# Local and global attention with a spectral feed-forward: loads on one queue, local denominators on TensorE alone, a layernorm's moments in the attention's slots

## The chip, the cores and the metric

The kernel runs on one core of a Trainium2 chip. The metric is the device time of one execution in microseconds. A core has a matrix engine (TensorE, PE in the profile; its weight loads are PEld), a vector engine (VectorE, DVE), an activation engine (ScalarE, ACT), a general engine (GpSimd, POOL) and a sync engine (SyncE, SP), each working through its own list of instructions in order. DMAs are issued from the lists of ACT and SP here, by instructions that can wait for semaphores like any others.

## What is computed

The input x is 2 x 8192 x 512 in float32. There are 16 heads of 32 channels and windows of 64 tokens.

```
y   = layernorm(x);  q, k, v = y @ w_qkv
loc = softmax(q . k of 64 keys around each query, 32 before to 31 after) @ v
glo = softmax(q . k of every 64th token of the whole sequence) @ v
x   = x + layernorm((loc + glo) @ w_out + b_out)
f   = real(ifft(fft(layernorm(x)) @ w_freq)) + bias
x   = x + layernorm(f)
```

The layernorms have no gain or shift. The Fourier transforms are folded into one 512 x 512 matrix at the start of the kernel, and matrix products split their operands into a high and a low part, three passes each.

## The kernel before

The program has three stages. The first projects q, k and v for 32 chunks of 512 tokens and stores them in DRAM (`qkd`, `kgd`, `vd`). The second is the attention, the third the residual and the feed-forward.

**Attention.** The work is cut into 128 units: 32 chunks times 4 groups (c) of 4 heads. The loop of line 884 runs over slots s. In one slot pieces of several units are laid out in the order of the string PLAN (line 822), which is an order written out by hand, and every engine follows it in its own list. The pieces are:

- `L0`, `L1`, `L2` (`load_unit`, line 147): four loads of queries (`qs`) and keys (`ks`) for unit s+3, issued from ACT's list (lines 167 and 169; line 173 for the global keys of a sequence's first chunk).
- `S` (`scores`, line 183), sixteen times: scores of unit s+2 on PE into one of three PSUM buffers, then two maxima on DVE (lines 200 and 203). `ne` (line 207) negates all the maxima at the slot's end, giving `mm`.
- `mx`, `sm`, `fm` for unit s+1: `mm` is transposed on PE (`pm`), copied on ACT (`mr`), stored from SP to DRAM (`md`, line 227) and loaded into four spare rows of `qs` (line 231). The load waits for the store.
- `g0`..`g3`, `a0`..`a3`, `b0`, `b1`, `k0`, `k1` for unit s: the products of the softmax on PE (into two PSUM buffers), their exponentials on ACT (line 625), and on POOL the selection of the window (line 675). The tile of local exponentials is `ptl`, that of global ones `ptg`.
- `ng`, `dg`, `n-`, `n0`..`n3`, `p0`, `p1`, `dl`, `de` for unit s-1: numerators and denominators. Denominators are matmuls with columns of ones. Each query has its local keys in two key blocks, so there are three pieces of `ptl` to be added. `p0` and `p1` (`gather`, line 727) first add two of them into `ptd`, one pair of heads on DVE and one on POOL; `dl` and `de` (`den_l`, line 737) then feed one piece of `ptl` and `ptd` to PE, 4 matmuls each.
- `dT`, `dI`, `t0`, `t1` on DVE (lines 761 to 775): the denominators are turned, inverted and spread (`dt`, `rc`, `rb`). `c0`, `c1`, `c2` on POOL multiply and add (`num`, `att`).
- `hs`, `ls`, `o0`..`o3`, `oe`, `ot` (class `Project`, line 787): a block of 128 tokens of an earlier chunk is split on ACT (`ath`) and DVE (`atl`), multiplied by `w_out` on PE (`po`; the third matmul of each three needs `atl`), given its bias on DVE (`t`, line 812) and stored from SP to DRAM (`td`, line 815).
- `va`, `vb`, `vc`: loads of the next chunk's values (`vh`, `vt`) from SP, in every fourth slot.

The PLAN of before:

```
L0 S S oe mx g0 L1 S S g1 p1 p0 a0 L2 ot c1 sm ng vg dg S S S a1 hs b0 k0 ls c2 S S va
n- n0 n1 n2 fm n3 dl de S S S g2 dT dI g3 vb t0 o0 S a2 o1 c0 S a3 t1 vc S o2 b1 k1 S o3 ne
```

After the last unit, the pieces that are left go into the list `rest`.

**Feed-forward.** 128 blocks of 128 tokens in groups of four go through nine steps (line 1066), one block a step, so that nine blocks and more are under way. `measure` takes the moments of the attention's output (`bn_stats` and `bn_aggr`, lines 108 and 109) from `t3r`, a ring of three chunks loaded from `td`, and POOL makes r1 and m1 of them at the group's end (`after_measure`, line 945). `residual` (line 989) adds to x, held in `x3r`, a ring of six chunks, and takes the moments of the sum. Then come `normalize` (ACT), `transpose` (PE, `pt`), `halves` (ACT `xh`, DVE `xl`), `ffn` (12 matmuls, `pf`), `last` (DVE), `spread` (ACT, squares) and `finish` (ACT, then an addition on POOL, line 1048). The last block of a chunk stores it (line 1054) and then loads the ring's next chunk into the place (line 915), which waits for the store. GAPS gives the least distance between steps of a block; a step in BATCHED waits for its whole group; PLACES orders the steps within one. Five pieces of `rest` are issued after each step.

Of the kernel before, what the change touches and what calls it, by code (L numbers as in the profile page):

```python
# [25 lines left out]
TB = 512  # L26
NB = TB // P
WIN = P + W
# [3 lines left out]
def kernel(  # L32
# [29 lines left out]
    nc = tc.nc  # L62
    B, N, C = x.shape
    DH = C // H
    KC = C // P
    R = P // DH
# [5 lines left out]
    KG = BACK + TB + HALF  # L72
    KW = KG + NG
# [11 lines left out]
    qkd = [[dram.tile([R, 4, DH, N], F32, name=f"qkd_{b}_{c}") for c in range(KC)] for b in range(B)]  # L85
    kgd = [dram.tile([KC, R, 2, DH, NG], F32, name=f"kgd_{b}") for b in range(B)]
# [19 lines left out]
    def stats(pool, mv, src, name):  # L106
        bs = pool.tile([P, 6], F32, tag="bs", name=f"bs_{name}", bufs=4)
        nc.vector.bn_stats(bs, src)
        nc.vector.bn_aggr(mv, bs)
# [4 lines left out]
    NU = len(units)  # L114
# [7 lines left out]
    ks, qbufs = [], []  # L122
# [24 lines left out]
    def load_unit(u, g):  # L147

        if not inside(u):
            return  # L150
        b, n, c = units[u]
        qs = QS[u] = qbufs[u % len(qbufs)]
        lo, hi = n * TB - BACK, (n + 1) * TB + HALF
        a, z = max(lo, 0), min(hi, N)
        if g == 0:
            if a > lo:
                nc.gpsimd.memset(ks[c][0:96, :, K0 : K0 + a - lo].bitcast(F32), 0.0)
            if z < hi:
                nc.gpsimd.memset(ks[c][0:96, :, K0 + z - lo : KG].bitcast(F32), 0.0)
        def heads(d, i, m):  # L160

            return d[:, i : i + m].rearrange("r i d t -> (i d) r t")

        def load(rows, i, m):
            rows = slice(rows, rows + m * DH)
            if i < 2:
                nc.scalar.dma_start(out=qs[rows].bitcast(F32), in_=heads(qkd[b][c][:, :, :, n * TB : (n + 1) * TB], i, m))
                return
            nc.scalar.dma_start(
                out=ks[c][rows, :, K0 + a - lo : K0 + z - lo].bitcast(F32), in_=heads(qkd[b][c][:, :, :, a:z], i, m)  # L170
            )
            if n == 0:
                nc.scalar.dma_start(out=ks[c][rows, :, KG:KW].bitcast(F32), in_=heads(kgd[b][c], i - 2, m))

        if g == 0:
            load(0, 0, 2)
        elif g == 1:
            load(DH, 2, 2)
        else:
            load(2 * DH, 0, 1)  # L180
            load(0, 2, 1)
# [54 lines left out]
    with ExitStack() as cx:  # L236
# [8 lines left out]
        xs, raw, spread, xT, kgs = {}, {}, {}, {}, {}  # L245
# [67 lines left out]
        with tc.tile_pool(name="setup", bufs=1, side="right") as sp:  # L313
# [124 lines left out]
            for d in range(KC):  # L438
# [3 lines left out]
                m = sp.tile([P, 2, C], F32R, tag="wf", name=f"wf_{d}")  # L442
# [3 lines left out]
                    out=wfd[:, d * P : (d + 1) * P, :].rearrange("i p o -> p i o"), in_=m.bitcast(F32)  # L446
# [6 lines left out]
        wk = cx.enter_context(tc.tile_pool(name="wk", bufs=2, side="right"))  # L453
# [116 lines left out]
    with ExitStack() as cx:  # L570
# [10 lines left out]
        ones = keep.tile([P, 2, DH], F32, name="ones")  # L581
# [31 lines left out]
        class Softmax:  # L613
# [4 lines left out]
            def __init__(self, u):  # L618
                self.u = u
                self.b, self.n, self.c = units[u]  # L620
                self.g, self.l, self.d = ([None, None] for _ in range(3))
                PT[u] = self

            def exp(self, dst, src):
# [99 lines left out]
                if m == NB - 1:  # L724
                    nc.scalar.copy(NUM[self.u][:, 1], self.nl)

            def gather(self, pair, eng):

                l = self.l[pair]
                d = self.d[pair] = wk.tile([P, 2, NB, W], F32, tag="ptd", name=f"ptd_{self.u}_{pair}", bufs=2)  # L730

                def part(at):
                    return bass.AP(tensor=l.tensor, offset=l.offset + at, ap=[l.ap[0], [WIN, 2 * NB], [1, W]])

                eng.tensor_tensor(d.rearrange("p i m w -> p (i m) w"), part(0), part(W), ALU.add)

            def den_l(self, half):

                ps = DEN[self.u].rearrange("p (m w) -> p m w", w=P)
                for r in range(R):  # L740
                    if half:
                        l = self.l[r // 2][:, r % 2]
                        rhs = bass.AP(tensor=l.tensor, offset=l.offset + 2 * W, ap=[l.ap[0], [WIN, NB], [1, W]])
                    else:
                        rhs = self.d[r // 2][:, r % 2]
                    nc.tensor.matmul(  # L746
                        ps[r * DH : (r + 1) * DH, :, half * W : (half + 1) * W],
                        ones[:, 1],
                        rhs,
                        start=False,  # L750
                        stop=True,
                        skip_group_check=True,
                    )

        class Finish:

# [30 lines left out]
        class Project:  # L787
# [22 lines left out]
            def bias(self):  # L810
                self.t = keep.tile([P, C], F32, tag="po", name=f"t_{self.i}", bufs=1)
                nc.vector.tensor_tensor(self.t, self.po, bo, ALU.add)

            def store(self):
                nc.sync.dma_start(out=td[self.k][self.j * P : (self.j + 1) * P, :], in_=self.t)

# [3 lines left out]


        PLAN = """
            L0 S S oe mx g0 L1 S S g1 p1 p0 a0 L2 ot c1 sm ng vg dg S S S a1 hs b0 k0 ls c2 S S va
            n- n0 n1 n2 fm n3 dl de S S S g2 dT dI g3 vb t0 o0 S a2 o1 c0 S a3 t1 vc S o2 b1 k1 S o3 ne
        """
        ENG = {k: nc.vector if e == "v" else nc.gpsimd for k, e in (t.split("=") for t in "p0=v p1=p c0=p c1=p c2=p".split())}
        plan = PLAN.split()
        wo = weights(keep, wod, "wo")
        bo = bias(keep, b_out, "bo")
        FIN = {}  # L830

        def slot(s):
# [20 lines left out]
            if inside(s - 1):  # L853
                v = PT.pop(s - 1)
                f = FIN[s - 1] = Finish(s - 1)
                ops |= {"ng": v.num_g, "dg": v.den_g, "n-": lambda: v.num_l(-1)}
                for m in range(NB):
                    ops[f"n{m}"] = lambda m=m: v.num_l(m)
                ops |= {"dl": lambda: v.den_l(1), "de": lambda: v.den_l(0)}
                for pair in range(R // 2):  # L860
                    ops[f"p{pair}"] = lambda pair=pair: v.gather(pair, ENG[f"p{pair}"])
                ops |= {"dT": f.turn, "dI": f.invert, "t0": lambda: f.spread(0), "t1": lambda: f.spread(1)}
                ops["c0"] = lambda: f.combine(0)
            if inside(s - 2):
# [7 lines left out]
                    ops[f"o{c}"] = lambda c=c: o.part(c)  # L872
            if inside(s - LAG - 1):
                z = PO.pop(s - LAG - 1)
                ops |= {"oe": z.bias, "ot": z.store}
            return ops

        LAG = KC + 2
# [20 lines left out]
    with ExitStack() as cx:  # L899
# [21 lines left out]
        class Group:  # L921
# [20 lines left out]
                nc.gpsimd.tensor_tensor(m, mv[:, :, 0:1], r, ALU.mult)  # L942
                return m

            def after_measure(self):
                self.r1 = self.rstd("r1", self.mv1[:, :, 1:2])
                self.m1 = self.moved("m1", self.mv1, self.r1)

            def after_residual(self):
                self.r2 = self.rstd("r2", self.mv2[:, :, 1:2])  # L950
# [15 lines left out]
        class Block:  # L966
# [14 lines left out]
                if self.i == self.g.n - 1:  # L981
                    getattr(self.g, f"after_{what}")()

            def measure(self):
                self.t = tring[self.k % len(tring)][:, self.j]
                self.stats("mv1", self.t)
                self.end("measure")

            def residual(self):
                self.x1 = xring[self.k % len(xring)][:, self.j]  # L990
                nc.vector.scalar_tensor_tensor(self.x1, self.t, self.g.r1[:, self.i], self.x1, ALU.mult, ALU.add)
                self.stats("mv2", self.x1)
                if self.j == NB - 1:
                    load_t3(self.k + len(tring))
                self.end("residual")
# [67 lines left out]
        groups = [Group(k, a, b) for k in range(NK) for a, b in zip(cuts[k], cuts[k][1:])]  # L1063
        blocks = [blk for g in groups for blk in g.blocks]

        STEPS = "measure residual normalize transpose halves ffn last spread finish".split()
        GAPS = dict(zip(STEPS, (0, 3, 2, 1, 1, 1, 1, 1, 2)))
        BATCHED = ("residual", "normalize", "spread", "finish")
        when, before = {}, [0] * len(blocks)
        for step in STEPS:  # L1070
            for i, blk in enumerate(blocks):
                at = i if step == "measure" else before[i] + GAPS[step]
                if step in BATCHED:
                    at = max(at, max(before[blocks.index(o)] for o in blk.g.blocks) + GAPS[step])
                if i and step != "measure":
# [6 lines left out]
        PLACES = "measure ffn halves last finish normalize spread residual transpose".split()  # L1082
# [95 lines left out]
```

## Time and profile before

| | us |
|---|---|
| median of 3 runs | 3813.4 (3806.15 to 3817.37) |
| profiled execution, its own time | 3819.91 |
| its span | 3818.2 |

Busy time over the span: PE 3462.0 us (91%), DVE 2591.0 (68%), POOL 1980.1 (52%), ACT 1664.8 (44%). The chain of waits follows the first stage's matmuls until 1080.9 us, and the attention's slots run from about 1131 to 3207 us. The feed-forward's first residual starts at 3270.7 us, the last one at 3768.8. In the profile L12 is line 12 of the kernel, a row `out<-in` names tiles with buffer numbers left out, and an idle time stands in square brackets with what ended it. A "chain of waits" is followed back from the last instruction of a stretch: at each step to what released it. "Busy PE" is modelled from the starts of matmuls, so it isn't PE at its peak. A float32 matmul stands in the trace as two records. "issue" is time in which an engine waited for nothing that the profile shows.

### The profile page before, as it was taken

The page shows a single profiled execution, that of the slowest core. Times are in us where ns is not written, and L with a number is a line of the kernel's source. Part 1 is how long each engine was busy: PE and PEld are TensorE (multiplying, and loading weights), DVE is VectorE, ACT ScalarE, POOL GpSimd, SP SyncE. Part 2 cuts the span into 40 slices and gives each one's busy share as a digit, 9 for nine tenths or more (in the row PEclk, how much of TensorE's full clock was granted, in tenths as well). Part 3 has the DMA queues.
Part 4 walks back from the last instruction along what each step waited for, and adds up shares of the span by engine and source line. Part 5 has one row for each costly group of instructions (what it writes and reads, how often), then busy time and mean ns, then how long its engine had stood idle before and what let it go on. Part 6 is the DMA issues. An engine that isn't in the chain of part 4 may idle for free.

```text
span 3818.2 us, 68772 instructions
## 1 busy us (share of the span) xinstructions
PE 3462.0 (91%) x23168; PEld 2569.3 (67%) x23168; DVE 2591.0 (68%) x9200; ACT 1664.8 (44%) x3711; POOL 1980.1 (52%) x2233
## 2 busy tenths in 40 slices
PE   7999999999997889998999989999989998788886
PEld 5778787888875566666666666666666665566665
DVE  5444344444445777777778877777778786788985
ACT  2222222222223445454545445454545454366666
POOL 2222222222213666666666666666666667266667
PEclk8999999999997999999999999999999999799998
DMA  7887887888876565656666565656565654355553
GB/s 236 236 240 233 238 243 235 240 238 238 240 207 167 127 153 148 160 147 153 154 149 159 143 148 148 157 149 156 147 161 147 161 146 136 119 188 200 198 199 131
DMA packets 355100, 685.05 MB, mean 179 GB/s; under 512 B 29729, under 2 KB 43681, under 8 KB 354242
## 3 DMA queue, kind: packets, MB, share of 16 engines
q1 hardware_dynamic: 244930, 454.13, 38.4%
q10 hardware_dynamic: 109824, 226.53, 25.4%
q8 instruction: 191, 3.13, 0.4%
q14 instruction: 155, 1.27, 0.1%
HBM read 436.08 MB, written 244.45 MB: 178 GB/s over the span
## 4 chain that ended last, share of the span: by engine, by line
PE 47%; DVE 25%; DMA 15%; ACT 4%; POOL 3%; SPq 2%; issue 2%; ACTq 1%; DVEq 0%; POOLq 0%
PE pp L98 15%; PE pv L98 6%; DVE junk L203 6%; PE s L199 5%; DVE mx L200 4%; DMA td<-t 4%; PE nl L693 4%; DMA x3r<-in_L_attn_x_dram 4%; DVE rb L775 4%; DMA out_dram<-x3r 3%; PE pa L628 3%; PE ng L693 3%; PE po L98 2%; PE den L693 2%; PE den L746 2%
## 5 line engine op out<-in xcount | busy, mean ns | idle before, releaser
L675 POOL TENSOR_SCALAR_AFFINE_SELECT ptl<-ptl 128x512 f32<-128x512 f32 (+1 forms) x768 | 629.3, 834 | 549.3 <-ACT ptl L625 531.8
L200 DVE TENSOR_REDUCE mx<-s 128x1 f32<-128x128 f32 x2048 | 576.8, 282 | 304.5 <-PE s L199 263.5
L203 DVE CUSTOM_DVE_ANT_0 junk<-s,mask 128x192 f32<-128x192 f32 x2048 | 709.7, 347 | 0.0
L98 PE MATMUL pp<-xT,wh 128*128 128x512 f32 x2048 | 649.4, 398 | 27.9 <-ACT xT L304 22.1
L199 PE MATMUL s<-ks,qs 96*128 96x384 f32 x1536 | 475.8, 381 | 82.4 <-DVE mx L203 74.6
L199 PEld LDWEIGHTS s<-ks,qs 96*128 96x128 f32 x1536 | 273.4, 191 | 321.7 <-issue 134.3
L780 POOL TENSOR_TENSOR num<-num,rb 128x512 f32<-128x512 f32 x256 | 386.1, 1508 | 177.3 <-DVE rb L775 177.3
L98 PEld LDWEIGHTS pp<-xT,wh 128*128 128x128 f32 x2048 | 388.6, 191 | 121.2 <-ACT xT L304 27.0
L625 ACT ACTIVATE ptl<-pa 128x384 f32<-128x384 f32 (+1 forms) x1024 | 337.2, 382 | 268.8 <-PE pa L628 254.4
L462 DVE TENSOR_TENSOR qk<-pp,qk 128x512 fp32r<-128x512 f32 x256 | 176.1, 689 | 380.9 <-ACT qk L461 372.4
L98 PE MATMUL pp<-xT,wl 128*128 128x512 f32 x1024 | 404.4, 395 | 0.0
L461 ACT CAST qk<-pp 128x512 fp32r<-128x512 f32 x256 | 149.6, 586 | 578.6 <-PE pp L98 415.3
L465 POOL CAST kgs<-qk 128x16 fp32r<-128x16 f32 x128 | 50.3, 393 | 669.9 <-DVE qk L462 669.9
L98 PE MATMUL po<-wo,ath 128*128 128x512 f32 x1024 | 350.6, 425 | 2.0 <-ACT ath L796 2.0
L625 ACT ACTIVATE ptg<-pg 128x512 f32<-128x512 f32 x512 | 276.4, 586 | 172.3 <-PE pg L628 169.9
L98 PE MATMUL pf<-wf,xh 128*128 128x512 f32 x1024 | 336.5, 410 | 0.0
L98 PE MATMUL pv<-wh,xT 128*128 128x512 f32 x1024 | 322.4, 390 | 0.0
L628 PEld LDWEIGHTS pa<-qs,ks 128*128 128x128 f32 x1536 | 242.8, 201 | 105.7 <-ACT ptg L625 90.7
L628 PE MATMUL pa<-qs,ks 128*128 128x192 f32 (+1 forms) x1536 | 254.0, 276 | 41.7 <-ACT ptg L625 41.0
L98 PE MATMUL pf<-wf,xl 128*128 128x512 f32 x512 | 215.6, 421 | 53.2 <-DVE xl L1012 47.6
L297 POOL TENSOR_TENSOR xt<-xt,spread 128x512 f32<-128x512 f32 x128 | 177.3, 1394 | 161.4 <-DVE xt L296 160.8
L98 PE MATMUL po<-wo,atl 128*128 128x512 f32 x512 | 213.1, 416 | 24.9 <-DVE atl L800 24.9
(161 smaller groups left out, 6831.6 us busy)
## 6 DMA issues: line engine op xcount, KB each, us to landing
qkd<-qk SPq DMA_DIRECT2D x512, 256.0 KB
ks<-qkd ACTq DMA_DIRECT2D x112, 640.0 KB
qs<-qkd ACTq DMA_DIRECT2D x128, 512.0 KB
ks<-qkd ACTq DMA_DIRECT2D x112, 320.0 KB
x<-in_L_attn_x_dram SPq DMA_DIRECT2D x32, 1024.0 KB
xt<-in_xt_dram SPq DMA_DIRECT2D x32, 1024.0 KB
vd<-v SPq DMA_DIRECT2D x128, 256.0 KB
qs<-qkd ACTq DMA_DIRECT2D x128, 256.0 KB
```

What stands on the lines that cost most here:

```text
L98: nc.tensor.matmul(ps, w, m, start=start and i == 0, stop=stop and i == len(terms) - 1)
L199: nc.tensor.matmul(ps[:, 0:w].rearrange("p (i w) -> p i w", i=2), q, both, start=True, stop=True)
L200: nc.vector.tensor_reduce(mx[:, j, 0, r : r + 1], ps[:, w - NG : w], AX.X, ALU.max)
L203: nc.vector.tensor_tensor_reduce(junk, ps[:, 0:WIN], fixed["mask"][:, variant, :], 1.0, LOWEST, ALU.add, ALU.max, mx[:, j, 1, r : r + 1])
L297: nc.gpsimd.tensor_tensor(t, t, r, ALU.mult)
L462: nc.vector.tensor_tensor(st[:, 2 * is_k + 1], pp, st[:, 2 * is_k], ALU.subtract)
L625: nc.scalar.activation(dst, src, AF.Exp, scale=SCALE)
L628: nc.tensor.matmul(ps, ks[self.c][:, r, lo : lo + m], QS[self.u][:, r, q0 : q0 + w], start=True, stop=True)
L675: nc.gpsimd.affine_select(part(at, w), part(at, w), [[0, 8], [step, w]], ALU.is_ge, 0.0, base=base, channel_multiplier=-step)
L693: nc.tensor.matmul(ps[r * DH : (r + 1) * DH, at], lhsT, rhs, start=start, stop=True, skip_group_check=True)
L775: nc.vector.transpose(self.rb[:, g], self.rc[:, g].unsqueeze(2).to_broadcast([P, TB // DH, DH]))
L780: ENG[f"c{g}"].tensor_tensor(num[:, g], num[:, g], self.rb[:, g], ALU.mult)
```

## The change

All loads of `load_unit` are issued from SP's list. `gather` is gone with `ptd`: `den_l` runs 12 matmuls, one for each of four heads and three pieces of `ptl`. The moments of the attention's output are taken in the slot, right from `t` in SBUF (`om`), and kept for all 128 blocks in one tile (`mvs`); the feed-forward's `measure` becomes `prepare`, which once a group makes r1 and m1 from it. `residual` no longer waits for its group, and its gap becomes 2. The PLAN is reordered: `L0` stands behind `sm`, `L1` and `L2` later, `fm` behind `L2` and the three scores after `dl`, `ls` between `dT` and `dI`, and `om`, `ot` and `sm` behind `a0`. The order of PE's products and scores among each other stays.

```diff
         def load(rows, i, m):
             rows = slice(rows, rows + m * DH)
             if i < 2:
-                nc.scalar.dma_start(out=qs[rows].bitcast(F32), in_=heads(qkd[b][c][:, :, :, n * TB : (n + 1) * TB], i, m))
+                nc.sync.dma_start(out=qs[rows].bitcast(F32), in_=heads(qkd[b][c][:, :, :, n * TB : (n + 1) * TB], i, m))
                 return
-            nc.scalar.dma_start(
+            nc.sync.dma_start(
                 out=ks[c][rows, :, K0 + a - lo : K0 + z - lo].bitcast(F32), in_=heads(qkd[b][c][:, :, :, a:z], i, m)
             )
...
-            def gather(self, pair, eng):
...
-                eng.tensor_tensor(d.rearrange("p i m w -> p (i m) w"), part(0), part(W), ALU.add)
-
-            def den_l(self, half):
+            def den_l(self):
                 ps = DEN[self.u].rearrange("p (m w) -> p m w", w=P)
-                for r in range(R):
-                    if half:
+                for half, src in ((1, 2 * W), (0, 0), (0, W)):
+                    for r in range(R):
                         l = self.l[r // 2][:, r % 2]
-                        rhs = bass.AP(tensor=l.tensor, offset=l.offset + 2 * W, ap=[l.ap[0], [WIN, NB], [1, W]])
-                    else:
-                        rhs = self.d[r // 2][:, r % 2]
-                    nc.tensor.matmul(
...
+                        nc.tensor.matmul(
+                            ps[r * DH : (r + 1) * DH, :, half * W : (half + 1) * W],
+                            ones[:, 1],
+                            bass.AP(tensor=l.tensor, offset=l.offset + src, ap=[l.ap[0], [WIN, NB], [1, W]]),
+                            start=False,
+                            stop=True,
+                            skip_group_check=True,
+                        )
...
+            def measure(self):
+                stats(keep, mvs[:, self.i], self.t, f"t{self.i}")
+
...
         PLAN = """
-            L0 S S oe mx g0 L1 S S g1 p1 p0 a0 L2 ot c1 sm ng vg dg S S S a1 hs b0 k0 ls c2 S S va
-            n- n0 n1 n2 fm n3 dl de S S S g2 dT dI g3 vb t0 o0 S a2 o1 c0 S a3 t1 vc S o2 b1 k1 S o3 ne
+            S S oe mx g0 S S g1 a0 om ot sm L0 c1 ng vg dg S S S L1 a1 hs b0 k0 c2 S S L2 n- n0 n1 n2 n3 dl
+            S S S fm g2 dT ls dI g3 va t0 o0 S a2 o1 c0 S a3 t1 vb S o2 b1 k1 S vc o3 ne
         """
...
-            def after_measure(self):
-                self.r1 = self.rstd("r1", self.mv1[:, :, 1:2])
-                self.m1 = self.moved("m1", self.mv1, self.r1)
+            def prepare(self):
+                at = self.k * NB
+                mv = mvs[:, at + self.j0 : at + self.j1]
+                self.r1 = self.rstd("r1", mv[:, :, 1:2])
+                self.m1 = self.moved("m1", mv, self.r1)
...
-            def measure(self):
-                self.t = tring[self.k % len(tring)][:, self.j]
-                self.stats("mv1", self.t)
-                self.end("measure")
+            def prepare(self):
+                if self.i == 0:
+                    self.g.prepare()
...
-        STEPS = "measure residual normalize transpose halves ffn last spread finish".split()
-        GAPS = dict(zip(STEPS, (0, 3, 2, 1, 1, 1, 1, 1, 2)))
-        BATCHED = ("residual", "normalize", "spread", "finish")
+        STEPS = "prepare residual normalize transpose halves ffn last spread finish".split()
+        GAPS = dict(zip(STEPS, (0, 2, 2, 1, 1, 1, 1, 1, 2)))
+        BATCHED = ("normalize", "spread", "finish")
```

More of the change, by code (lines that the diff above doesn't have):

```diff
@@ L172, in load @@
             if n == 0:
-                nc.scalar.dma_start(out=ks[c][rows, :, KG:KW].bitcast(F32), in_=heads(kgd[b][c], i - 2, m))
+                nc.sync.dma_start(out=ks[c][rows, :, KG:KW].bitcast(F32), in_=heads(kgd[b][c], i - 2, m))
         if g == 0:
@@ L620, in __init__ @@
                 self.b, self.n, self.c = units[u]
-                self.g, self.l, self.d = ([None, None] for _ in range(3))
+                self.g, self.l = [None, None], [None, None]
                 PT[u] = self
@@ L725, in num_l @@
                     nc.scalar.copy(NUM[self.u][:, 1], self.nl)
-            def gather(self, pair, eng):
[L729 to L733, printed above, removed]
-                eng.tensor_tensor(d.rearrange("p i m w -> p (i m) w"), part(0), part(W), ALU.add)
-            def den_l(self, half):
+            def den_l(self):
                 ps = DEN[self.u].rearrange("p (m w) -> p m w", w=P)
-                for r in range(R):
-                    if half:
+                for half, src in ((1, 2 * W), (0, 0), (0, W)):
+                    for r in range(R):
                         l = self.l[r // 2][:, r % 2]
-                        rhs = bass.AP(tensor=l.tensor, offset=l.offset + 2 * W, ap=[l.ap[0], [WIN, NB], [1, W]])
-                    else:
-                        rhs = self.d[r // 2][:, r % 2]
[L746 to L753, printed above, removed]
+                        nc.tensor.matmul(
[6 more added lines that the diff above has]
+                        )
         class Finish:
@@ L822 @@
         PLAN = """
-            L0 S S oe mx g0 L1 S S g1 p1 p0 a0 L2 ot c1 sm ng vg dg S S S a1 hs b0 k0 ls c2 S S va
-            n- n0 n1 n2 fm n3 dl de S S S g2 dT dI g3 vb t0 o0 S a2 o1 c0 S a3 t1 vc S o2 b1 k1 S o3 ne
+            S S oe mx g0 S S g1 a0 om ot sm L0 c1 ng vg dg S S S L1 a1 hs b0 k0 c2 S S L2 n- n0 n1 n2 n3 dl
+            S S S fm g2 dT ls dI g3 va t0 o0 S a2 o1 c0 S a3 t1 vb S o2 b1 k1 S vc o3 ne
         """
-        ENG = {k: nc.vector if e == "v" else nc.gpsimd for k, e in (t.split("=") for t in "p0=v p1=p c0=p c1=p c2=p".split())}
+        ENG = {k: nc.vector if e == "v" else nc.gpsimd for k, e in (t.split("=") for t in "c0=p c1=p c2=p".split())}
         plan = PLAN.split()
@@ L829 @@
         bo = bias(keep, b_out, "bo")
+        mvs = keep.tile([P, NU, 2], F32, name="mvs")
         FIN = {}
@@ L858, in slot @@
                     ops[f"n{m}"] = lambda m=m: v.num_l(m)
-                ops |= {"dl": lambda: v.den_l(1), "de": lambda: v.den_l(0)}
-                for pair in range(R // 2):
-                    ops[f"p{pair}"] = lambda pair=pair: v.gather(pair, ENG[f"p{pair}"])
+                ops["dl"] = v.den_l
                 ops |= {"dT": f.turn, "dI": f.invert, "t0": lambda: f.spread(0), "t1": lambda: f.spread(1)}
@@ L874, in slot @@
                 z = PO.pop(s - LAG - 1)
-                ops |= {"oe": z.bias, "ot": z.store}
+                ops |= {"oe": z.bias, "om": z.measure, "ot": z.store}
             return ops
@@ L982, in end @@
                     getattr(self.g, f"after_{what}")()
-            def measure(self):
-                self.t = tring[self.k % len(tring)][:, self.j]
-                self.stats("mv1", self.t)
-                self.end("measure")
+            def prepare(self):
+                if self.i == 0:
+                    self.g.prepare()
             def residual(self):
                 self.x1 = xring[self.k % len(xring)][:, self.j]
+                self.t = tring[self.k % len(tring)][:, self.j]
                 nc.vector.scalar_tensor_tensor(self.x1, self.t, self.g.r1[:, self.i], self.x1, ALU.mult, ALU.add)
@@ L1071 @@
             for i, blk in enumerate(blocks):
-                at = i if step == "measure" else before[i] + GAPS[step]
+                at = i if step == "prepare" else before[i] + GAPS[step]
                 if step in BATCHED:
                     at = max(at, max(before[blocks.index(o)] for o in blk.g.blocks) + GAPS[step])
-                if i and step != "measure":
+                if i and step != "prepare":
                     at = max(at, when[step, i - 1] + (step not in BATCHED or blk.g is not blocks[i - 1].g))
@@ L1081 @@
             before = [when[step, i] for i in range(len(blocks))]
-        PLACES = "measure ffn halves last finish normalize spread residual transpose".split()
+        PLACES = "prepare ffn halves last finish normalize spread residual transpose".split()
         todo = defaultdict(list)
```

## The prediction

> **What bounds the kernel now.** I read the busy tenths first, then busy time by stage, then in each stage the chain of waits, then the timeline where one slot of the chain is longer than its neighbours. Busy time by stage (columns: stretch, its length, busy us of PE, PE's weight loads, DVE, ACT, POOL, granted clock, DMA share, GB/s), here the steady parts of the attention and of the feed-forward:
>
> ```profile
> core 0: us, PE busy (x) PEld busy (x) DVE busy (x) ACT busy (x) POOL busy (x), PEclk, DMA share, GB/s
> 1282.20:3090.00 1807.80, 1644.52 (x14337) 1159.27 (x14336) 1410.06 (x6385) 907.26 (x2240) 1178.47 (x1147) 0.98 0.61 152
> 3296.00:3745.00 449.00, 400.85 (x1825) 296.17 (x1825) 407.53 (x914) 300.79 (x550) 292.88 (x442) 0.99 0.53 183
> ```
>
> The first row is 112 slots of 16.14 us each, PE 91% busy; in the second DVE is at 91% and PE at 89%. Shares settle nothing where two engines are this close, so the chain of waits of one ordinary slot (start, us, what):
>
> ```profile
> 2028.93 0.21 DVE mm L211
> ...
> 2036.88 0.86 PE den L746 x16
> 2037.74 0.39 PE s L199
> ...
> 2039.67 0.64 DVE dt L765
> ...
> 2044.02 0.23 DVE mm L211
> ```
>
> A slot is the time from one negation of the maxima (mm) to the next, 15.09 us. It has two halves. From mm to about 2038.1 the chain is pm, mr on ACT, one exponential and then PE without a break, through the local denominators (den, line 746) to the next scores. From 2038.15 to 2044.5 it is DVE without a break: seven maxima pairs at 0.475 us, dt, rc, two rb, mm. Whatever is added to PE before that s, or to DVE after it, lengthens the slot.
>
> The starts of mm around it are 1994.8, 2013.16, 2028.93, 2044.02: slots of 18.4, 15.8, 15.1, and 15.1 again to 2059.1. This pattern of four (one token chunk) is found through the stage. The timeline of the long slot, and ls (atl) in it and in the next:
>
> ```profile
> 2002.81 0.58 ACT L703 COPY num<-ng 128x512 f32<-128x512 f32 x1 [4.60 <-PE nl L693]
> ...
> 2004.49 0.69 DVE L800 TENSOR_TENSOR atl<-att,ath 128x512 fp32r<-128x512 f32 x1 [3.26 <-ACT ath L796]
> ...
> 2020.57 0.69 DVE L800 TENSOR_TENSOR atl<-att,ath 128x512 fp32r<-128x512 f32 x1 [0.32 <-ACT ath L796]
> ```
>
> ACT stood 4.60 us before a copy, its exponentials and ath came late, DVE stood 3.26 us before atl. The load of ks just ahead of the copy on ACT's queue was issued only at 2002.40. ACT's waits (line, what for: us, times, longest) name what it waited for, a store on the other queue, not PE:
>
> ```profile
> ACT num L703 <- DMA td<-t: 48.5, 10, 5.3
> ```
>
> It happens in the slot that also loads vh and vt. In the feed-forward the chain is a loop through the x3r ring:
>
> ```profile
> 3450.70 5.67 DMA x3r<-in_L_attn_x_dram
> ...
> 3458.19 0.59 DVE bs_mv L108
> ...
> 3459.39 1.04 POOL r L936
> ```
>
> Its period is 15.7 us a chunk: load 5.67, residual and its moments 1.8, moments of the attention's output 0.59+0.19 (the step that is moved), POOL's r and m for it 0.25+1.04+0.38, POOL's last addition 1.26, the store 4.3, and gaps. Where DVE has less to do, at the end of the program, PE alone sets the pace:
>
> ```profile
> 3766.52 0.44 PE pt L1006 x4
> 3766.96 2.83 PE pf L98 x12
> ```
>
> That is 3.25 us a block, 13.0 a chunk.
>
> **Loads to SyncE.** Four issues a slot (0.62, 0.60, 0.32, 0.51 us) leave ACT's queue. I give these issues themselves no worth: in the ordinary slot ACT's exponential starts at 2030.39, just before mr ends at 2030.48, although an issue runs from 2030.14 to 2030.74, so they lie beside ACT's work. The Trainium skill (DMA: Bandwidth & Descriptors, "Issuing engines are not separate DMA queues") speaks against the move: transfers of all issuing engines share the same DMA engines, and several issuers only save issue time. By that rule the move is worth 0. But the row above is a wait for a completed transfer that stands ahead of an issue, and what is behind it on ACT stands too. By the row, the long slot loses its excess, 18.4-15.1 = 3.3 us, and its follower 0.7: 4.0 us a chunk. I take the row. On SP the wait may return; behind it then are the remaining loads and the fold of the maxima, not exponentials.
>
> Cover on SP: the four issues sum to 2.05 us a slot. In the order after, SP is held by sm's wait for mr (the store md came 2.4 us after mm), then issues the loads, then fm waits for md (666.7 us over 127 times, 5.2 each). Behind sm now stand loads due at the next slot's first scores, behind fm the vh and vt loads, due a slot later. One slot's traffic ahead of fm's transfer is 1.73 MB of loads and 0.29 of stores; 152 GB/s at a share of 0.61 is 249 GB/s when busy, so 8.1 us. From 2 us after mm this ends at about 10, fm lands by 12 to 14. g0 of the next slot needs it 16.9 us after mm. I take no wait; bounds 0 and 2 us a slot. Loads of the first units, issued in the projection: 0, bounds -5 and +10 us in all, since ACT's and SP's waits there are for PE and DVE.
>
> **Denominators.** Per slot: DVE loses a sum (ptd) of 0.69 us, POOL one of 1.27, PE goes from 8 matmuls to 12. Sixteen records (8 matmuls) took 0.86 us in the chain, so 4 more take 0.43, ahead of the scores that DVE waits for: +0.43 on the path. Nothing hides it. POOL's 1.27 us is off the path in a steady slot. In the drain (3214 to 3235, selections on POOL end to end) it saves some 4 us in all.
>
> **Moments in the slots (om).** bn_stats and its aggregate take 0.79 us (3453.07 to 3453.86). They stand almost where ptd stood, ahead of the idle 1.39 us in which DVE waits at 2033.84 for scores: 0.1 longer than ptd, hidden, cost 0. Without that cover it would be 0.1 a slot. om issues no transfer.
>
> **ls behind dT.** atl moves from the PE half, where DVE had 0.84 us to spare before the next scores (and stood 0.32 for ath), into the DVE half: 0.61 us net of overlap, less a gap of 0.03: +0.58. Also o0's third matmul needs atl. Before, it started 1.1 us after DVE's first maximum of this half (2039.24 against 2038.15). After, atl is there 2.8 us after it (three maxima 1.52, dt 0.63, atl 0.61). PE stands some 1.7 us, and the scores behind it come about when DVE wants them. Bounds of this: 0 and 0.5 us a slot; I take 0.1.
>
> **Sum, attention.** 15.09 + 0.43 + 0.58 + 0.1 = 16.2 us in every slot, against a mean of 16.14: what the long slots give back, the ordinary ones spend. With the bounds, 16.05 to 16.6. For 128 slots +8 us (-12 to +58).
>
> **Sum, feed-forward.** DVE's block goes from 3.59 us (xl to xl, 3450.27 to 3453.86) to 2.80. The loop loses 0.59+0.19+0.25+1.04+0.38 = 2.45 us a chunk: 13.2. PE gives 13.0. So 13.2, and 449 us hold 28.6 chunks of 15.7: 28.6 x 2.5 = -71 us. prepare still issues POOL's r and m, once a chunk at another step, where its input has long been there. residual no longer waits for its group of four, so the first feed-forward matmul stands 4 block steps earlier. But 3250 to 3293 is a serial chain of output projections with the td store (12.04 us behind prefetches), which stays: I take -8 us (0 to -13). With the drain's 4: -83.
>
> **Total.** -83 + 8 = -75 us against the profiled execution's 3819.9 (span 3818.2): 3745. That execution was 6.5 above the median of 3813.4, so against the median 3738; I say 3740.
>
> **Rivals.**
> *The ring stays the bound* (0.14). Transfers packed into 13 us instead of 15.7 raise 183 GB/s to 218. The load took 5.67 us beside another load, and could take 7, the store 5: the loop is then 15.2 and gives 0.5 x 28.6 = 14 us. That is 57 less than forecast: 3797. For it: every chunk's residual waits for the x3r load. Against it: the ring's distance in steps is unchanged and DVE's slack per block rises to 0.45 us.
> *The DVE half isn't the bound after all* (0.08): atl and the denominators are absorbed, every slot is 15.3. That is 128 x 0.9 = 115 us less than forecast: 3625. Against it: the chain shows no gap there.
> *Slower: the fold waits behind the loads* (0.10). In one queue qs<-md is behind 1.73 MB. The Trainium skill (same page, "Queues, rings and completion order") says that a DMA engine goes round the queues that have work, packet by packet; one queue takes this turn-taking from the fold. The trace has one case: td<-t at 3250.34, behind prefetches in its own queue, took 12.04 us where others in the chain took about 6. At 6 the fold, issued 7.8 us after mm as now, lands at 13.8, in time: cost 0. At 12 it lands at 19.8, 2.9 us after it is due. At half of that, 1.4 us x 128 = 180 us: 3920. It decides once the fold is over 0.6 us late in each slot (75/128). Against it: md goes ahead of the loads and should land sooner than the 4.9 us it took among them.
> *The move doesn't do what it says*: ACT still waits for the store by another road, the long slots stay 3.3 longer. 30 x 3.3 = 99 us more than forecast: 3840. It has part of the 0.10.
>
> **Numbers.** Likeliest 3740 (0.68, its own range 3700 to 3785), ring 3797 (0.14), absorbed 3625 (0.08), slower cases 3840 to 3920 (0.10). The range 3692 to 3800 holds the first two. A measurement tells 0.3%, 11 us, from no change: faster below 3802, slower above 3825. Faster 0.86, same 0.06, slower 0.08.
>
> **What would show it.** Slots even, 16.0 to 16.5 us, without ACT's wait for td; den with 24 records and about 1.3 us in the chain; DVE's half near 7.0 us; feed-forward chunks near 13.2 us with PE above 95%. Wrong: long slots every fourth, PE pg waiting for DMA qs<-md, slots of 15.3, or a feed-forward that still waits for x3r with 15 us a chunk.

## The result: slower, where faster was forecast

The changed kernel takes 3912.5 us (median of 4 runs, 3909.1 to 3914.2), the kernel before 3810.8 beside it: a ratio of 1.0264, 95% interval 1.0246 to 1.0283, or 102 us more. The forecast was 3740, the range 3692 to 3800. Its profiled execution has a span of 3907.3 us. The page's busy times, of after:

```profile
PE 3448.6 (88%) x24192; PEld 2576.0 (66%) x24192; DVE 2567.6 (66%) x9072; ACT 1669.2 (43%) x3711; POOL 1738.5 (44%) x2105
```

PE (modelled), DVE and POOL were busy for less time than before (3462.0, 2591.0 and 1980.1 us), in a longer span: the loss is in waits. Where it lies is seen by the first and the last mm, of before and of after (row of line 211: ns min/median/max, start of the first and of the last in us):

```profile
L211 DVE TENSOR_SCALAR mm<-mx x128: 181/213/924, 1130.9 to 3206.6; 128x32 fp32r<-128x32 f32 x128
```

```profile
L211 DVE TENSOR_SCALAR mm<-mx x128: 182/859/866, 1130.3 to 3361.4; 128x32 fp32r<-128x32 f32 x128
```

From the first mm to the last, the attention went from 2075.7 to 2231.1 us: +155. What lies behind the last mm went from 611.6 to 545.9: -66. (The two make 89 us, where the medians differ by 102: the profiled execution of before took 9 us more than its median, that of after 3 us less.) The same row has the first surprise: mm itself, an instruction on 32 elements, went from 0.21 to 0.86 us.

Busy time by stage, steady parts, after (columns as before):

```profile
core 0: us, PE busy (x) PEld busy (x) DVE busy (x) ACT busy (x) POOL busy (x), PEclk, DMA share, GB/s
1283.00:3099.90 1816.90, 1548.72 (x14146) 1078.82 (x14145) 1368.85 (x6033) 848.07 (x2080) 897.47 (x963) 0.99 0.61 140
3460.00:3820.00 360.00, 343.82 (x1694) 280.51 (x1693) 300.68 (x635) 280.36 (x517) 271.08 (x408) 1.00 0.61 215
```

PE fell from 91% to 85% in the attention and rose from 89% to 96% in the feed-forward. By the starts of mm the slots are even now, 17.33 us, except for ten of 18.9; every fourth slot is no longer long. Each of the ten holds a stretch of 3.4 us in which the granted TensorE clock is 0.50, and from 1283 us to the last mm no other slot does. One of these stretches and the 3.4 us before it (columns as above):

```profile
1924.60:1928.00 3.40, 1.88 (x12) 1.26 (x8) 2.82 (x12) 1.08 (x2) 1.78 (x2) 1.00 1.09 251
1928.00:1931.40 3.40, 3.40 (x12) 3.02 (x12) 1.62 (x6) 0.66 (x2) 1.28 (x1) 0.50 1.02 284
```

PE was busy for 1.88 of the 3.4 us ahead of it. The ten cost 16 us together, (18.9 - 17.33) x 10, and don't explain the loss: before had 25 such stretches from 1283 us to its last mm. ACT's waits for td are gone. So one forecast came true, and the level at which the slots became even is wrong: 17.33 instead of 16.2. The chain of waits of an ordinary slot, after:

```profile
2029.04 1.29 PE den L733 x24
2030.33 0.39 PE s L199
...
2032.25 0.63 DVE dt L752
2032.88 0.58 DVE atl L787
2033.47 0.04 issue
2033.51 0.50 PE po L98
```

The denominators take 1.29 us in place of 0.86: +0.43, as forecast. atl stands in DVE's half with 0.58, as forecast. What is new is that the chain leaves DVE there and goes through PE's po, which it didn't touch in the ordinary slot of before. PE's row, and then DVE's rows, in the same slot:

```profile
2033.51 0.50 PE L98 MATMUL po<-wo,atl 128*128 128x512 f32 x1 [1.53 <-DVE atl L787]
```

```profile
2035.38 0.29 DVE L200 TENSOR_REDUCE mx<-s 128x1 f32<-128x128 f32 x1 [0.39 <-PE s L195]
...
2037.77 0.86 DVE L211 TENSOR_SCALAR mm<-mx 128x32 fp32r<-128x32 f32 x1
2038.66 0.19 DVE L212 SCALAR_TENSOR_TENSOR mm<-mx,mm 128x32 fp32r<-128x32 f32 x1
```

PE stands 1.53 us before o0's third matmul. All its later work of the slot is late, so DVE waits 0.39 us for a score (and 0.14 for a later one). At the end mm takes 0.86 us. POOL's rows show what runs at that time:

```profile
2037.50 2.48 POOL L675 TENSOR_SCALAR_AFFINE_SELECT ptl<-ptl 128x1024 f32<-128x1024 f32 x3 [1.60 <-ACT ptl L625]
```

The first of these three selections has 1024 elements a partition and takes 1.09 us (mean of its form), so it ends about 2038.59; mm ends at 2038.63. I compared the two ends in 110 slots of either kernel: mm always ends 0.03 to 0.04 us after the end of a selection. POOL's row of before:

```profile
2043.11 2.48 POOL L675 TENSOR_SCALAR_AFFINE_SELECT ptl<-ptl 128x1024 f32<-128x1024 f32 x3 [0.25 <-ACT ptl L625]
```

There mm began at 2044.02, with 0.2 us of the first selection left. After, mm begins 0.27 us into it.

The growth of an ordinary slot adds up over three stretches. From the end of mm's second instruction (line 212) to DVE's first maximum after den: 8.80 to 9.22 us, +0.42 (den). From there to mm's start: 5.87 to 7.03, +1.16 (atl 0.58, waits 0.53, and 0.05 that no row accounts for). mm's own time: +0.65. Sum 2.23, and 17.33 - 15.10 = 2.23.

### The profile page after: what moved, and what is told of

Same layout as the page of the kernel before. It is cut to its first block, busy times and chain, and to the rows that moved or that the text cites. A ratio compares the mean times of both kernels' runs of the same rounds, so it can differ in the third digit from the quotient of the medians.

```text
span 3907.3 us, 70102 instructions
## 1 busy us (share of the span) xinstructions
PE 3448.6 (88%) x24192; PEld 2576.0 (66%) x24192; DVE 2567.6 (66%) x9072; ACT 1669.2 (43%) x3711; POOL 1738.5 (44%) x2105
## 3 DMA queue, kind: packets, MB, share of 16 engines
q1 hardware_dynamic: 354754, 680.65, 65.0%
## 4 chain that ended last, share of the span: by engine, by line
PE 56%; DVE 15%; DMA 11%; issue 7%; ACT 4%; SPq 4%; POOL 3%; POOLq 0%; ACTq 0%; DVEq 0%
PE pp L98 13%; PE po L98 6%; PE pv L98 6%; PE s L199 5%; PE nl L693 4%; PE pa L628 4%; PE den L733 4%; PE ng L693 3%; DVE junk L203 3%; DVE mx L200 3%; PE den L693 3%; DMA vt<-vd 2%; PE pb L628 2%; PE s L195 2%; PE pf L98 2%
## 5 line engine op out<-in xcount | busy, mean ns | idle before, releaser
L675 POOL TENSOR_SCALAR_AFFINE_SELECT ptl<-ptl 128x512 f32<-128x512 f32 (+1 forms) x768 | 610.7, 810 | 798.8 <-ACT ptl L625 781.4
L767 POOL TENSOR_TENSOR num<-num,rb 128x512 f32<-128x512 f32 x256 | 327.3, 1279 | 334.3 <-DVE rb L762 333.9
L199 PE MATMUL s<-ks,qs 96*128 96x384 f32 x1536 | 437.9, 373 | 19.6 <-DMA ks<-kgd 10.1
L98 PE MATMUL po<-wo,atl 128*128 128x512 f32 x512 | 222.2, 434 | 213.5 <-DVE atl L787 213.5
L98 PE MATMUL po<-wo,ath 128*128 128x512 f32 x1024 | 337.9, 412 | 1.1 <-ACT ath L783 1.1
L98 PEld LDWEIGHTS po<-wo,atl 128*128 128x128 f32 x512 | 99.2, 194 | 287.0 <-DVE atl L787 269.3
```

What stands on the lines that cost most here:

```text
L98: nc.tensor.matmul(ps, w, m, start=start and i == 0, stop=stop and i == len(terms) - 1)
L199: nc.tensor.matmul(ps[:, 0:w].rearrange("p (i w) -> p i w", i=2), q, both, start=True, stop=True)
L675: nc.gpsimd.affine_select(part(at, w), part(at, w), [[0, 8], [step, w]], ALU.is_ge, 0.0, base=base, channel_multiplier=-step)
L767: ENG[f"c{g}"].tensor_tensor(num[:, g], num[:, g], self.rb[:, g], ALU.mult)
```

## The experiments

Each was timed beside the kernel before on the same chip; the medians of before were 3810.8 to 3814.1 us, and a ratio is that of the runs side by side, not of the medians in the column. "Slot" is the most frequent distance between two starts of mm, "all slots" the time from the first mm to the last, both of the profiled execution.

| kernel | us, median | ratio to before, 95% interval | slot | all slots |
|---|---|---|---|---|
| before | 3810.8 | 1 | 15.10, every fourth mostly 18 to 19 | 2075.7 |
| after | 3912.5 | 1.0264 (1.0246 to 1.0283) | 17.33 | 2231.1 |
| after, ls back | 3711.4 | 0.9717 (0.9695 to 0.9739) | 15.53 | 2044.7 |
| after, mm by tensor_reduce | 3874.7 | 1.0154 (1.0137 to 1.0171) | 17.12 | 2193.0 |
| after, selection after mm | 3830.8 | 1.0050 (1.0033 to 1.0067) | 16.66 | 2154.8 |
| the same, o0 later | 3760.0 | 0.9867 (0.9845 to 0.9889) | 16.16 | 2079.0 |
| after, loads from ACT | 3938.3 | 1.0324 (1.0296 to 1.0351) | 17.34, some 19 to 20 | 2264.3 |
| after, PLAN of before | 3693.5 | 0.9687 (0.9665 to 0.9709) | 15.53 | 2013.0 |
| before, ls moved only | 3927.6 | 1.0310 (1.0283 to 1.0337) | 16.9 | 2185.5 |
| before, loads only | 3703.2 | 0.9701 (0.9684 to 0.9719) | 15.10 | 1963.1 |
| before, denominators only | 3836.3 | 1.0052 (1.0033 to 1.0071) | 15.54, every fourth mostly 17 to 18 | 2089.8 |
| before, moments only | 3752.0 | 0.9843 (0.9825 to 0.9860) | 15.10, every fourth mostly 18 to 19 | 2075.3 |
| before, loads and moments | 3644.1 | 0.9557 (0.9534 to 0.9580) | 15.10 | 1963.7 |

The theory after the two traces were compared: the place of ls costs what is too much, by three terms (atl itself, PE's stand, mm behind POOL's selection). The rivals were the queue (loads or the fold of the maxima late) and the denominators.

**ls back at its old place in the changed kernel.**

```diff
-a1 hs b0 k0 c2 S S L2 n- n0 n1 n2 n3 dl S S S fm g2 dT ls dI g3
+a1 hs b0 k0 ls c2 S S L2 n- n0 n1 n2 n3 dl S S S fm g2 dT dI g3
```

> The changed kernel with ls back at its old place (behind k0, ahead of c2), nothing else. Theory ls: of the 2.24 us by which an ordinary slot grew (15.09 to 17.33), 1.16 are in DVE's half (atl itself 0.58, and waits for scores because PE stands 1.5 us before the third matmul of o0) and 0.65 are mm, which grew from 0.21 to 0.86 because it now meets POOL's first selection of the slot's end. Both come from ls; the slot falls to about 15.5 us, the feed-forward stays, the whole near 3680 us. Rival queue: the loads on SP or the fold behind them hold the slot; then it stays at 17 us or above and the whole above 3880. Rival denominators: they hold more than 0.43; slot above 16.3.

The slot fell to 15.53 us, the whole to 3711: one word in the PLAN is 201 us. Both rivals fall. The whole is 31 us over the 3680 expected, because some slots take 16 to 19 us. Of this kernel's waits between 1283 and 3000 us, this one is for its loads:

```profile
PE s L199 <- DMA ks<-qkd: 25.5, 19, 3.1
```

So the later places of the loads in the new PLAN do leave scores without keys, once the slots are short enough; at 17.33 us no such wait is in the list. The halved clock has a part in it: all 11 slots over 17 us in that time hold a stretch at 0.50, most of them just behind a wait of 1.6 to 3.1 us for keys, and slots with a shorter wait and no stretch are at most 16.4.

**The negation of the maxima by another kind of instruction.**

```diff
-nc.vector.tensor_scalar_mul(mm[:, :, 0], flat, -1.0)
+nc.vector.tensor_reduce(mm[:, :, 0], flat.unsqueeze(3), AX.X, ALU.max, negate=True)
```

> The changed kernel with one instruction in place of another: the negation of the maxima (mm, line 211) is made by a tensor_reduce over an axis of one element with a negated output, in place of a tensor_scalar; the same values. Theory port: the tensor_scalar waits for the end of POOL's running selection (in all 110 slots looked at its end lies 0.03 to 0.04 us before the selection's end), an instruction of another kind does not, so mm takes 0.2 to 0.3 us in place of 0.86 and the slot 16.7 us in place of 17.33: the whole near 3830 us. Rival: mm waits for something else that happens to end with the selection (a semaphore, its own data): mm or the gap before it keeps 0.86, the whole stays at 3912.

(In that text a direction is wrong: mm ends 0.03 to 0.04 us after the selection, not before it.) The result is half a miss: line 211 took 0.19 us, but the slot only fell to 17.12, and the whole to 3875 instead of 3830. DVE's rows say where it went, and POOL's row what runs then:

```profile
2032.17 0.19 DVE L211 TENSOR_REDUCE mm<-mx 128x32 fp32r<-128x32 f32 x1
2032.39 0.65 DVE L212 SCALAR_TENSOR_TENSOR mm<-mx,mm 128x32 fp32r<-128x32 f32 x1
```

```profile
2031.91 2.43 POOL L675 TENSOR_SCALAR_AFFINE_SELECT ptl<-ptl 128x1024 f32<-128x1024 f32 x3 [1.60 <-ACT ptl L625]
```

The wait moved to the next instruction, which takes 0.65 us in place of 0.19 and ends at 2033.04, again with the first selection. The Trainium skill has this rule (SBUF — State Buffer, "Who interferes with whom"): DVE and POOL share a pair of ports under an exclusive lock; a tensor_scalar in a two-port mode takes it, a DVE instruction with two SBUF inputs meets POOL's reads, a tensor_reduce meets neither. The rows agree in all three: 0.86 for the tensor_scalar, 0.65 for the instruction with two inputs, 0.19 for the tensor_reduce, under the same selection. No row shows the mode of this tensor_scalar, or the ports.

**POOL's last selection held until mm is written.** This takes the cause away, not the instruction.

```diff
-... S o2 b1 k1 S vc o3 ne
+... S o2 b1 S vc o3 ne kw k1
+def after_mm():
+    t = wk.tile([1, 1], F32, tag="kw", name=f"kw_{s}")
+    nc.gpsimd.tensor_copy(t, MX[s + 2][0:1, NB - 1, 1, 2 * R - 1 : 2 * R].bitcast(F32))
```

> The changed kernel with POOL's last selections of a slot (k1) held until the negated maxima are written, by a copy of one element of mm on POOL ahead of them; k1 stands behind ne in the PLAN. Theory port: then neither line 211 nor line 212 can meet a running selection; mm takes 0.2 us and its second half 0.19, and the slot falls from 17.33 by 0.65 to 16.7: the whole 3830. With the tensor_reduce the wait had gone over to line 212 (0.19 to 0.65) and only 0.21 was won. Rival: something else ends at that time too (PE's last projection matmuls), and the slot stays above 17.0: the whole above 3870.

Slot 16.66, whole 3831. Lines 211 and 212 of this kernel:

```profile
L211 DVE TENSOR_SCALAR mm<-mx x128: 181/181/183, 1131.7 to 3286.5; 128x32 fp32r<-128x32 f32 x128
L212 DVE SCALAR_TENSOR_TENSOR mm<-mx,mm x128: 191/192/193, 1131.9 to 3286.7; 128x32 fp32r<-128x32 f32 x128
```

No instance is long any more, and the slot gives back 0.67 us. The third term is shown, by taking away what it met.

**Beside that, o0 behind S and a2.**

```diff
-t0 o0 S a2 o1 c0 S a3
+t0 S a2 o0 o1 c0 S a3
```

> The run that held POOL's last selections until mm is written, and beside that o0 behind S and a2 in the PLAN, so that PE has more to do before the third matmul of o0 needs atl. Theory: the 0.5 us of waits in DVE's half (0.39 and 0.14 before two maxima in the changed kernel) go, the slot falls from 16.65 to 16.1, which is what the prediction's sum gave for the path without them (15.09 + 0.43 + 0.58): 3760 us. Rival: the waits move to another score and the slot stays above 16.5: 3815 or more.

Slot 16.16, whole 3760. The 0.5 us are PE's stand before atl as DVE feels it. With the stand the halved clock is gone too: from 1283 us to the last mm this kernel has no stretch at 0.50, the one above with the stand has 13. What remains over 15.10 are den (0.43) and atl (0.58): the prediction's sum of 16.1, which thus held for a PLAN that the change didn't have.

**ls moved in the kernel before, nothing else.**

```diff
-a1 hs b0 k0 ls c2 S S va ... g2 dT dI g3
+a1 hs b0 k0 c2 S S va ... g2 dT ls dI g3
```

> The kernel before with ls moved behind dT, as in the change's PLAN, and nothing else. Theory: ordinary slots grow by atl's 0.58 us in DVE's half, about 0.5 of waits behind PE's stand before the third matmul of o0, and up to 0.65 for mm meeting POOL's selection: 16.2 to 16.9 us. The long slots' excess may shrink, as DVE no longer stands for ath. The whole 3860 to 3930. Rival: ls costs only together with the other parts; the whole stays within 20 us of 3811.

Slots of 16.9, 3928 us: +113, without any other part of the change. mm has a median of 0.86 us here too:

```profile
L211 DVE TENSOR_SCALAR mm<-mx x128: 181/859/2035, 1132.6 to 3318.0; 128x32 fp32r<-128x32 f32 x128
```

That is 1.8 us a slot (16.9 - 15.1) for one instruction of 0.58. POOL's selection begins 6.75 us after DVE's first maximum here, as after the change (6.76), and with ls back at its old place 4.96, as before: the place of ls alone moves it.

**The loads alone**, from SP in the kernel before (both `nc.scalar.dma_start` of `load_unit`, and the one for the global keys, to `nc.sync`).

> The kernel before with the loads of load_unit issued from SP in place of ACT, the PLAN as before. Theory: the long slot of every four (18.4 us) and its follower (15.8) fall to 15.1 to 15.4, since ACT no longer stands at an issue: 3.7 to 4 us a chunk, the whole near 3690 us. Rival queue: the fold's transfer behind the loads in one queue is late, slots of 16 us and more, the whole above 3810.

Slots of 15.1, 3703 us: -110 (0.9701). The whole excess of the long slots is gone, 113 us of attention time (2075.7 to 1963.1). ACT's waits of 48.5 us for td are no longer in the list, and DVE's wait for ath fell from 117.6 us between 1600 and 3200 us to this:

```profile
DVE atl L800 <- ACT ath L796: 39.4, 97, 4.2
```

But two things went together. In before, ACT stands 4.5 to 6.5 us ahead of the copy (`num`, line 703) in all 26 long slots between 1283 and 3000 us, whatever the profile names as the releaser. In 21 of them a stretch of 3.4 us or more at half the granted clock follows, and in no other slot. Two long slots of before, in which ACT stood 4.60 and 4.61 us (columns as in the table by stage):

```profile
1994.80:2013.16 18.36, 15.72 (x128) 11.40 (x128) 12.44 (x58) 7.95 (x20) 9.78 (x11) 0.91 0.74 187
2059.13:2076.25 17.12, 14.46 (x129) 10.10 (x128) 12.26 (x58) 7.95 (x20) 10.13 (x11) 1.00 0.80 200
```

The follower is 15.44 us on average behind a long slot without a stretch, 15.86 behind one with it. So the stand alone is worth (17.12 - 15.10) + (15.44 - 15.10) = 2.4 us a chunk, and the halved clock 1.24 + 0.42 = 1.66 more. With the loads on SP two such stretches are left of 25, and the granted clock over a whole execution is 0.974 to 0.976 in all runs, where the runs of before have 0.964 to 0.967. As an estimate, some 40 of the 113 us are the clock (25 x 1.66) and some 70 the stand. The move took both away; that the stand brings the halved clock is likely from where it falls, but no run separates them.

**The loads back on ACT in the changed kernel** (the reverse edit).

> The changed kernel with its loads issued from ACT again. Theory: the move to SP is a gain here too, as it was alone: ACT's waits at issues come back, in some slots at least, 1 to 4 us a chunk, the whole 3940 to 4040 us. Rival queue: part of the 17.33 us comes from SP's queue; then the run is faster than 3912.

3938 us, 26 slower than with the loads on SP (the expectation's lower end was 3940). Most slots stay at 17.34 us, some take 19 to 20. Waits for DMAs, of which the changed kernel's list has none between 1283 and 3000 us, are there, if not the one for td:

```profile
PE s L199 <- DMA ks<-qkd: 15.3, 11, 2.0
...
ACT num L725 <- DMA md<-mr: 4.9, 3, 1.8
ACT num L725 <- DMA qs<-md: 4.0, 1, 4.0
```

The profile of this run has 21 stretches at half the clock in its slots, against 10 with the loads on SP; at the 1.57 us that each cost there that is 17 us of the difference. So the move is a gain in both PLANs, worth 110 us in one and 26 in the other, and the queue on SP is no part of the 17.33 us.

**The denominators alone in the kernel before** (gather removed, `den_l` of the change, `p1 p0` and `de` out of the PLAN).

> The kernel before with 12 matmuls for the local denominators in place of two sums and 8 matmuls, all else as before. Theory: 0.43 us more on PE ahead of the scores that DVE waits for, in every slot: ordinary slots 15.5, long slots as before, the whole near 3865 us. Rival: the sums taken from DVE and POOL pay for it, ordinary slots stay at 15.1 and the whole within 10 us of 3811.

A miss in size: 3836, +0.5% (0.3 to 0.7), instead of 3865. Ordinary slots grew by 0.44, as expected, but the long ones shrank from mostly 18 to 19 us to mostly 17 to 18. The profile says why in part: between 1283 and 3000 us 9 of 26 long slots hold a stretch at half the clock, where before had 21. Like against like they hardly changed: 17.12 to 17.36 us without a stretch, 18.90 to 18.80 with one. So in the attention 14 us remain of 55. Fewer stretches (11 for 25 over all slots) make some 23 us of the missing 41, estimated at the 1.66 us from above; part of the rest is PE's added work that lies beside ACT's stand. Why the stretches are fewer here, no run shows. Behind the last mm 4.5 us were won, about what the prediction gave for POOL's sums in the drain. (The profiled execution, 3829 us, is the shortest of this kernel's five.)

**The moments alone in the kernel before** (`om` behind `a0`, `mvs`, `prepare`, steps and gaps of the change).

> The kernel before with the moments in the slot (om behind a0) and prepare in the feed-forward, nothing else. Theory: the feed-forward gives what it gave beside the loads (3644 against 3703): 59 to 66 us, the whole near 3750. Rival: in slots where ACT stands, DVE is late and om adds to it: up to 0.8 us in one slot of four, 25 us, the whole near 3775.

3752, -61 us (0.9843). All slots 2075.3 against 2075.7: om costs the attention nothing. Behind the last mm: 611.6 to 544.4. The wait of ACT that the loads bring is untouched (1283 to 3000 us):

```profile
ACT num L703 <- DMA td<-t: 52.7, 11, 5.3
```

**The change's three parts in the PLAN of before.**

```diff
+L0 S S oe mx g0 L1 S S g1 a0 om L2 ot c1 sm ng vg dg S S S a1 hs b0 k0 ls c2 S S va
+n- n0 n1 n2 fm n3 dl S S S g2 dT dI g3 vb t0 o0 S a2 o1 c0 S a3 t1 vc S o2 b1 k1 S o3 ne
```

> All three parts of the change, but in the order of the PLAN of before (loads at L0, L1, L2's old places, ls behind k0, fm among the numerators; om behind a0, dl in one piece). Theory: slots 15.1 + 0.43 = 15.55 us, all even, since the loads are issued early: 3675 us, 40 under the run with ls alone moved back (3711), whose slots of 17 to 19 us come from loads that landed late for the scores. Rival: those long slots come from one queue as such, and stay: 3710.

3693, between the two expectations. In the attention it is most of the theory's 40 us: all slots 2013.0 us against 2044.7 with ls back alone, no wait for a DMA is left in the list between 1283 and 3000 us, and one stretch at half the clock in place of 14. But what lies behind the last mm took 551.6 us here and 535.7 there. Over the kernels with the moments in the slot this part lies between 535.7 and 555.3 us; I have no cause for that spread.

**Loads and moments, without the denominators.**

The loads are issued from SP, the steps of the feed-forward are those of the change, and in the PLAN of before:

```diff
-g1 p1 p0 a0 L2 ot
+g1 p1 p0 a0 om L2 ot
```

> The kernel before with two of the change's three parts: loads from SP, and the moments taken in the slot (om behind a0) with prepare in the feed-forward. The sums of the exponentials, 8 matmuls for the denominators and the rest of the PLAN stay as before. Theory: the parts add: slots of 15.1 to 15.2 us as with the loads alone (3703), and the feed-forward's 66 us less, as in the changed kernel: near 3637 us. Rival: om, with the sums still on DVE, lengthens the slot by up to 0.79 us: up to 3738.

3644 us, 0.9557 (0.9534 to 0.9580): 170 us faster than before beside it (3814.1) and 268 faster than the change. The two parts add (110 + 61 = 171). It is the fastest version found.

## Why the prediction was wrong, step by step

**Failed: "ls behind dT".** The prediction put it at 0.58 for atl and 0.1, with bounds 0 and 0.5, for PE's stand before o0. atl was 0.58. The stand was seen ("some 1.7 us"; it is 1.53), but the scores behind it were judged to come "about when DVE wants them". They came 0.39 and 0.14 us later: the term lies at its upper bound. And a term is missing from the sum: mm behind POOL's selection, 0.65 us in each slot, which was put at nothing. The trace of before had it in plain sight, in the timeline of the long slot, where mm took 0.86 us, and in the row of line 211, with a longest of 924 ns against a median of 213. I read the chain's "DVE mm" of 0.87 us there and took it for a part of that slot's trouble. The sum should have asked which instruction on the path has two prices, what decides between them, and on which side the moved instruction leaves it. PE's stand makes b1 late, and with it POOL's selection: 4.96 us after DVE's first maximum in the half before the change, 6.76 after, so mm fell into the front of the selection instead of its end. Missing in all: 0.43 us of waits (0.53 for 0.1) and 0.65 of mm a slot, (0.43 + 0.65) x 128 = 138 us, where the attention missed by 147 (+155 for +8). The sum's range was also too narrow: its lower end, 16.05, is below what its own terms give (15.09 + 0.43 + 0.58 = 16.10), and the 2 us a slot that were allowed for the fold aren't in its upper end.

**The loads: right that the long slots go, the size in part by luck.** The row (ACT standing for a completed transfer) was right against the rule that separate issuers only save issue time: 4.0 us a chunk were forecast, 128 us; the run with the loads alone won 113 in the attention. But the long slot's 3.3 us and the follower's 0.7 were put down to the stand alone, and 1.2 and 0.4 of them are the halved clock, which the prediction didn't look at. The number held because the move took both. The issues themselves were given no worth; no run tells them from the waits.

**Right: the denominators' 0.43 us** a slot. The forecast of no wait for the fold held: no wait for qs<-md stands in the list of the changed kernel's steady slots, and one of 1.8 us in all, in two places, in that of the loads alone. So the slower rival was wrong about the place: the queue did no harm to the fold, and the loss came from a moved instruction. That 3912 lies inside this rival's 3840 to 3920 is chance.

**Right: om costs nothing**, shown alone.

**The feed-forward: the mechanism right, the size small.** Forecast -83 with the drain, measured -66. The chain of waits there, after:

```profile
3576.68 1.26 POOL x3r L1039
...
3581.17 4.25 DMA out_dram<-x3r
...
3585.43 5.51 DMA x3r<-in_L_attn_x_dram
```

The loop through the ring is still in the chain, now with PE's matmuls and the second layernorm's POOL steps between the transfers. By the starts of residual, chunks alternate between some 12 and 15.5 us, 13.8 on average over 26 of them, where 13.2 was forecast and 15.7 was before: (13.8 - 13.2) x 28.6 = 17 us, as much as the miss; the two small terms (-8 and -4) weren't told apart. The rival "the ring stays the bound" gave 15.2; the truth lies between, with transfers that didn't become slower (4.25 and 5.51 against 4.3 and 5.67).

**Not settled:** what halves the clock for 3.4 us. In the changed kernel and in before, PE had stood idle for much of the 3.4 us ahead of such a stretch (busy, as modelled, for 55% of it in the one, 17 to 53% in the other), and the run without PE's stand has none; but no run changes that alone. Also open are why ACT's list waited for a store ahead of a load, and the spread of the feed-forward's time among kernels that are alike in it.

## What to carry to other kernels

A step moved on one engine moves everything that waits for it: follow it to its reader (here PE's third matmul), and from there to what that reader lets another engine start (here POOL's selection), before its own 0.58 us is taken for its price. When an instruction on the path shows two durations in a trace, find out what decides between them; it is a wait that is booked as work. Where single slots are longer than the rest, read the granted clock in them before a wait is charged with all of it. And test the parts of a change apart: here two of three were worth 170 us together, and one word of the PLAN hid that.

## What the runs showed of the hardware

- A tensor_scalar on DVE over 32 elements a partition waits for the end of a POOL selection that began before it, and the trace shows it as a long instruction, not as idle time: 0.18 us became 0.86 in nearly every slot. With a tensor_reduce in its place (0.19 us) the wait passed to the next instruction, which has two SBUF inputs (0.19 to 0.65).
- A DMA issue on ACT lies beside running activations (an issue of 0.60 us under an mr of 0.58 delayed nothing), but a wait ahead of an issue holds all activations behind it: ACT stood 4.5 to 6.5 us in every fourth slot, and moving the loads off ACT won 110 us in this kernel.
- With all loads, stores and small transfers in one queue (680.65 MB), the waits for the small fold were none in the steady slots of one kernel and 1.8 us in all in another.
- The granted TensorE clock fell to 0.50 for 3.4 us at a time behind stands of PE: 25 times in the slots of before, 10 in those of after, none in the run without PE's stand. One such stretch cost 1.2 to 1.6 us of its slot.
